# Projections of an attention layer in three float32r passes of split operands instead of a seven-product block scheme

## Chip, cores and metric

The kernel runs on one core of one Trainium2 chip. The metric is the device time of one execution in microseconds, the median of three runs.

## The reference

Two residual layers with layer norms work on `x` of shape 64 x 256 x 512 in float32. The first is a graph layer, the second an eight-head attention with a mask from the same adjacency matrix:

```python
mi = jnp.einsum('bkd,od->bko', x, Wi);  mj = jnp.einsum('bkd,od->bko', x, Wj)
out = deg[None, :, None] * (mi + b) + jnp.einsum('ij,bjo->bio', a, mj)
h = _layernorm(x + out)
...
q, k, v = (split_heads(h @ W.T + b) for W, b in ((Wq, bq), (Wk, bk), (Wv, bv)))
scores = jnp.where(mask, -jnp.inf, jnp.einsum('bhqd,bhkd->bhqk', q, k) * scale)
out = jnp.einsum('bhqk,bhkd->bhqd', jax.nn.softmax(scores, axis=-1), v)
y = _layernorm(h + merge_heads(out) @ Wo.T + bo)
```

The four projections (q, k, v, and o, the output projection) are the part that is changed. Each is a product of 256 x 512 rows per batch with a 512 x 512 matrix.

## The kernel before

The batches are worked on in 32 pairs (`NB = 2`, `NG = 32`). The outer loop is `for g in range(NG - 1)`. One turn holds, in the order in which PE gets it: the attention of pair `g` (scores, exponentials, values, sums `den`) in four steps of two head pairs, with the graph layer of pair `g + 1` (`layer0`) put in between; then the handover; then o of pair `g` and q, k and v of pair `g + 1`, and the first two scores of that pair. The last pair's o is done at the end of the kernel in plain float32 matmuls.

In a projection the two batches of a pair are the two row blocks of one 2 x 2 block matrix, and the weight matrix is another. `pair_steps` does the product of the two in seven block products (Winograd's form of Strassen's scheme) instead of eight; `left_steps` makes the four sums `S1` to `S4` of the left side, `make_factors` the four differences `T1` to `T4` of the weights, once, and stores them in device memory. Each block product is four float32 matmuls of 256 columns, named `st` after their bank in the profile. Each needs one weight block `factor`, 256 KB, which is loaded anew for every pair: 28 loads for a pair. The loads are issued on SP's queue (L442, `bring`) as slots of a ring of nine come free; the order is the list `queue`.

On its way from the graph layer to the projections `h` has to be turned, so that its features lie along the partitions. For the first pair that is done on PE (`h_transpose`). For all others `send_h` writes each row tile to device memory (`h_cols`, L603), reads the whole batch back in another layout (`hB`, L607), and `turn_h` turns it on DVE with a stream transpose of 128 x 1024 (L485).

The handover of a turn starts with the last `values`. `divide_two` copies the unnormalised output from PSUM on ACT, sums the exponentials on PE (`den`), takes the reciprocal on DVE (L886, `rden`), spreads it over the partitions by eight small DMAs on SP (L894, `spread`), and `multiply` on POOL (L848) multiplies. In the same stretch the second batch of the next pair gets the last part of its graph layer: `neighbours` (the matmuls `pa`, whose operands `graph`, `hi` and `lo` are float32r), `take` (L579, add and statistics on DVE, `rstd` on POOL), `give` (L467, normalisation on ACT) and `send_h`. For one batch `take(1)`, `take(0)`, `give(1)`, `give(0)` stand for its two row tiles. `take(1)` of the second batch starts with `add_scaled` (L521).

The order of instructions on an engine is the program's where the code says `in_order`; a scheduler orders the others. [...]

Of the kernel before, what the change touches and what calls it, by code (L numbers as in the profile page):

```python
# [16 lines left out]
P = 128  # L17
# [207 lines left out]
def unshifted_path(ctx, tc, flag, x, adj, wiT, wjT, b0, wqT, bq, wkT, bk, wvT, bv, woT, bo, out):  # L225
# [27 lines left out]
    AHEAD = 8  # L253
# [6 lines left out]
    p4 = ctx.enter_context(tc.tile_pool(name="p4", bufs=4))  # L260
    p6 = ctx.enter_context(tc.tile_pool(name="p6", bufs=6))
    stream = ctx.enter_context(tc.tile_pool(name="stream", bufs=AHEAD + 1))
# [40 lines left out]
    b_bc = p4.tile([P, D], F32, tag="u", name="b_bc")  # L303
# [20 lines left out]
    xT, xS, hT, hS, qT, kT, vv, aoT, oS = ({} for _ in range(9))  # L324


    ident = const.tile([P, P], F32, name="ident")
# [15 lines left out]
    aT = p3.tile([P, NT, N], F32, tag="pk", name="aT")  # L343
    deg = small.tile([P, NT], F32, tag="deg", name="deg")
# [16 lines left out]
    def check_graph():  # L361


        exact = p1.tile([P, NT, N], F32, tag="oS", name="exact")
        in_order(nc.vector.tensor_tensor(exact, aT, graph.bitcast(F32), ALU.not_equal))
        in_order(nc.vector.tensor_reduce(inexact, exact.rearrange("p t n -> p (t n)"), AX.X, ALU.max))
        in_order(nc.vector.tensor_scalar(maskT, aT, 0.0, MASK, ALU.is_equal, ALU.mult))
# [9 lines left out]
    def load_bias(b, name):  # L377
        t = const.tile([P, NC], F32, tag=name, name=name)
        nc.sync.dma_start(out=t, in_=b)
        d = const.tile([P, 2], F32, tag=name + "d", name=name + "d")  # L380
        return t, d

    bq_sb, bqd = load_bias(bq, "bq")
    bk_sb, bkd = load_bias(bk, "bk")

    def bias_steps():
        for t, d in ((bq_sb, bqd), (bk_sb, bkd)):
            in_order(nc.vector.tensor_sub(d, t[:, 2:4], t[:, 0:2]))

    bv_t = small.tile([P, NC], F32, tag="bvt", name="bv_t")  # L390
# [5 lines left out]
    def blocks_of(w):  # L396
        return (w.rearrange("(h c p) (j o) -> p h c j o", h=2, p=P, j=2) if w is woT else
                w.rearrange("(p h c) (j o) -> p h c j o", h=2, p=P, j=2))

    sources = {}  # L400
    for name, w in (("wq", wqT), ("wk", wkT), ("wv", wvT), ("wo", woT)):
        src = blocks_of(w)
        sources[name] = {B11: src[:, 0, :, 0], B21: src[:, 1, :, 0], B22: src[:, 1, :, 1]}


    def load_raw(w, tag):
        raw = p1.tile([P, 2, 2, 2, H], F32, tag=tag, name="raw")
        nc.sync.dma_start(out=raw.rearrange("p h c j o -> p (h c) (j o)"),
                          in_=w.rearrange("(c p) o -> p c o" if w is woT else "(p c) o -> p c o", p=P))
        return raw  # L410

    def make_factors(w, name, raw):
        kept = dram.tile([4, P, 2, H], F32, tag=name, name=name)
        t1, t2, t3, t4 = (p4.tile([P, 2, H], F32, tag="u", name="t") for _ in range(4))
        b11, b12, b21, b22 = (raw[:, h, :, j, :] for h in range(2) for j in range(2))
        for n, (t, p, m) in enumerate(((t1, b12, b11), (t2, b22, t1), (t3, b22, b12), (t4, b21, t2))):
            in_order(nc.vector.tensor_sub(t, p, m))
            nc.sync.dma_start(out=kept[n], in_=t)
        sources[name].update({T1: kept[0], T2: kept[1], T3: kept[2], T4: kept[3]})

    spread = p3.tile([P, NC, P], F32, tag="pk", name="spread")
# [3 lines left out]

    def fold_value_bias(raw):

        pb = score_bank("pb")
        for c in range(NC):
            h, kc = divmod(c, 2)  # L430
            matmul(pb, spread[:, c], raw[:, h, kc].rearrange("p j o -> p (j o)"),
                   start=(c == 0), stop=(c == NC - 1))
        nc.vector.tensor_add(bo_bc, pb, bo_bc)
# [4 lines left out]
    def bring():  # L438
        if queue:
            name, n = queue.pop(0)  # L440
            f = stream.tile([P, 2, H], F32, tag="factor", name="factor")
            nc.sync.dma_start(out=f, in_=sources[name][n])  # L442
            coming.append(f)

    def next_factor():
        f = coming.pop(0)
        bring()
        return f


    def norm_stats(t, order=anywhere):
# [3 lines left out]
        nc.vector.bn_aggr(mv, st)  # L455
        ve = small.tile([P, 1], F32, tag="ve", name="ve")
        nc.vector.tensor_scalar(ve, mv[:, 1:2], EPS, None, ALU.add)
# [3 lines left out]
        nc.gpsimd.tensor_tensor(rstd, ve, mhalf, ALU.pow)  # L461
# [40 lines left out]
    def l0_steps(b, late=False):  # L502
# [21 lines left out]
        def split(t):  # L524
            nc.scalar.copy(k["hi"][:, t, :], k["mj"][:, t, :])
            nc.gpsimd.tensor_tensor(k["lo"][:, t, :], k["mj"][:, t, :], k["hi"][:, t, :].bitcast(F32),
                                    ALU.subtract)
# [13 lines left out]
        def step4():  # L541
            product("y", xS[b]["S2"], T2, True)
            nc.vector.tensor_add(keeper("u2"), banks["y"], k["u1"])

        def step5():
            product("z", xS[b]["S1"], T1, True)
            k["mj"] = p1.tile([P, NT, D], F32, tag="mj", name="mj")
            nc.vector.tensor_copy(k["mj"][:, 1, :], banks["z"])

        def step6():  # L550
            product("y", xS[b]["S3"], T3, False)
            nc.vector.tensor_add(keeper("u3"), banks["y"], k["u1"])
            nc.gpsimd.tensor_tensor(k["mj"][:, 1, :], k["mj"][:, 1, :], k["u3"], ALU.add)
# [34 lines left out]

    def new_h(g):
        hT[g] = p1.tile([P, NC, NB * N], F32, tag="hT", name="hT")  # L590
        hS[g] = pair_blocks(hT[g], "hS")

    def sum_h(g):
        for step in left_steps(hS[g], in_order):
            step()
# [3 lines left out]
    def send_h(b, t):  # L599
        i = b % NB  # L600
        if t == 1:
            h_cols[b] = dram.tile([D // P, N, P], F32, tag=f"h{i}", name="h_cols")
        nc.sync.dma_start(out=h_cols[b][:, t * P:(t + 1) * P, :].rearrange("q p n -> p q n"),  # L603
                          in_=xh[b][:, t, :].rearrange("p (q n) -> p q n", n=P))
        if t == 0:
            hB[b] = p1.tile([P, N // R, P], F32, tag="hB", name="hB")
            nc.sync.dma_start(out=hB[b].rearrange("p a n -> p (a n)"),  # L607
                              in_=h_cols[b].rearrange("q (r a) n -> (q r) (a n)", r=R))

    def turn_h(b):  # L610
        g, i = divmod(b, NB)
        if i == 0:
            new_h(g)
        transposed(hT[g][:, :, i * N:(i + 1) * N], hB.pop(b))
        if i == NB - 1:
            sum_h(g)

    def h_transpose(b, t, borrow=False):
# [4 lines left out]
        pt = (score_banks("pt_h")[:, 0, :] if borrow else bank("pt_h")).rearrange("p (c n) -> p c n", c=NC)  # L623
        for c in range(NC):
            transpose(pt[:, c, :], xh[b][:, t, :].rearrange("p (n c) -> p c n", c=NC)[:, c, :], ident)
        nc.scalar.copy(hT[g][:, :, i * N + t * P:i * N + (t + 1) * P], pt)  # L626
        if t == 0 and i == NB - 1:
            sum_h(g)
# [6 lines left out]
    def pair_blocks(m, tag):  # L635

        s = p1.tile([P, 4, 2, N], F32, tag=tag, name=tag)
        return left_blocks(m[:, 0:2, 0:N], m[:, 2:4, 0:N], m[:, 0:2, N:2 * N], m[:, 2:4, N:2 * N], s)

    def block_product(bank, left, right, flip, first):  # L640


        for m in range(2):
            ms = slice(m * P, (m + 1) * P)
            for kc in range(2):
                lhsT, rhs = (right[:, kc, ms], left[:, kc, :]) if flip else (left[:, kc, ms], right[:, kc, :])
# [471 lines left out]
```

## Time and profile before

| | |
|---|---|
| median of 3 runs | 3070.91 us (3069.15 to 3071.65) |
| profiled execution | 3068.79 us |
| its span | 3066.9 us |
| PE, matmuls | 3036.6 us, 99% |
| DVE | 2178.3 us, 71% |
| POOL | 1519.5 us, 50% |
| ACT | 974.1 us, 32% |
| DMA moved | 447.54 MB, 146 GB/s on average |
| granted TensorE clock | 0.999 |

"Busy" is the union of an engine's instructions. Since matmuls overlap in the array, the mean duration of one is longer than its share of PE's time; what a matmul costs is read from start to start. A duration is in us unless marked ns. The column after the second bar of a group is the time for which the engine stood idle just before these instructions, and who released it. A DMA's time runs from its issue to its landing; DMA issues are listed under the queue of the engine that issues them (SPq for SP).

### The profile page before, as it was taken

The numbers are of one execution on the slowest core, as the hardware profiler recorded it, in microseconds if no ns is written. First come the engines' busy times: TensorE is split into PE (matmuls) and PEld (weight loads), VectorE is DVE, ScalarE is ACT, GpSimd is POOL, SyncE is SP. The second block draws the span as 40 slices with busy tenths as digits, with TensorE's granted clock in tenths as the row PEclk, the third lists the DMA queues.
The fourth block names the chain that finished last, engine by engine and source line by source line (L and its number), as shares of the span: only waits on it lengthen the run. The fifth ranks groups of instructions, "written<-read, shape, count | busy, mean of one in ns | idle before, by whom it ended". The sixth has DMA issues, their size and how long they took to land. (4 is left out here: it accounts for less than half of the span.)

```text
span 3066.9 us, 46810 instructions
## 1 busy us (share of the span) xinstructions
PE 3036.6 (99%) x16646; PEld 2124.6 (69%) x16646; DVE 2178.3 (71%) x3298; ACT 974.1 (32%) x1861; POOL 1519.5 (50%) x1255
## 2 busy tenths in 40 slices
PE   7999999999999999999999999999999999999998
PEld 4667766677766777666776667776677766677665
DVE  6776677766777667777677777677766777767775
ACT  2323333323333333332233332333333333323332
POOL 2544545544545445464454554454544546445453
PEclk9999999999999999999999999999999999999999
DMA  7455544455444555345553445544455444555333
GB/s 255 123 151 159 169 121 136 132 161 166 144 125 127 159 170 155 116 133 154 161 168 119 126 145 160 167 134 134 127 158 170 151 121 128 159 161 166 120 111 96
DMA packets 410411, 447.54 MB, mean 146 GB/s; under 512 B 40896, under 2 KB 300224, under 8 KB 409792
## 3 DMA queue, kind: packets, MB, share of 16 engines
q1 hardware_dynamic: 410176, 444.50, 48.8%
q8 instruction: 136, 2.23, 0.3%
q14 instruction: 99, 0.81, 0.1%
HBM read 340.79 MB, written 70.25 MB: 134 GB/s over the span
## 5 line engine op out<-in xcount | busy, mean ns | idle before, releaser
L461 POOL TENSOR_TENSOR rstd<-ve,mhalf 128x1 f32<-128x1 f32 x256 | 140.5, 552 | 707.3 <-DVE below L459 707.3
L816 POOL TENSOR_TENSOR pk<-pe 128x512 f32<-128x512 f32 x256 | 323.1, 1278 | 322.2 <-ACT pe L813 322.2
L290 PE MATMUL po<-w,xS 128*128 128x512 f32 x1024 | 462.2, 599 | 0.7 <-DVE xS L478 0.7
L290 PE MATMUL st<-hS,factor 128*128 128x256 f32 x2048 | 453.2, 379 | 1.5 <-DVE u L689 1.2
L290 PEld LDWEIGHTS st<-hS,factor 128*128 128x128 f32 x2048 | 388.4, 190 | 56.3 <-DVE xh L744 1.7
L813 ACT ACTIVATE pe<-pe 128x1024 f32<-128x1024 f32 x256 | 270.8, 1058 | 364.4 <-DVE pe L809 364.4
L290 PE MATMUL po<-w,xT 128*128 128x512 f32 x768 | 352.1, 601 | 14.8 <-DVE xS L477 9.3
L290 PE MATMUL st<-hT,factor 128*128 128x256 f32 x1536 | 352.5, 379 | 0.7 <-ACT hT L626 0.7
L290 PEld LDWEIGHTS po<-w,xS 128*128 128x128 f32 x1024 | 189.6, 190 | 235.6 <-issue 206.3
L809 DVE TENSOR_TENSOR pe<-ps,maskT 128x1024 f32<-128x1024 f32 x256 | 298.0, 1195 | 35.4 <-PE ps L290 35.4
L290 PEld LDWEIGHTS st<-hT,factor 128*128 128x128 f32 x1536 | 291.9, 190 | 41.8 <-ACT hT L626 0.9
L886 DVE RECIPROCAL rden<-den 128x256 f32<-128x256 f32 x127 | 222.5, 1752 | 76.6 <-PE den L290 73.6
L290 PEld LDWEIGHTS po<-w,xT 128*128 128x128 f32 x768 | 144.2, 191 | 181.9 <-issue 162.8
L887 POOL TENSOR_TENSOR rtot<-rtot,rden 128x256 f32<-128x256 f32 x127 | 106.8, 841 | 320.1 <-DVE rden L886 320.1
L290 PE MATMUL ps<-qT,kT 64*128 64x256 f32 x2048 | 265.0, 393 | 0.0
L290 PE MATMUL pav<-pe,v_sb 128*32 128x256 f32 x4096 | 248.4, 382 | 1.9 <-ACT pe L813 1.9
L290 PEld LDWEIGHTS ps<-qT,kT 64*128 64x128 f32 x2048 | 184.5, 186 | 78.1 <-issue 38.6
L744 DVE TENSOR_TENSOR xh<-st,xh 128x512 f32<-128x512 f32 x186 | 144.5, 777 | 132.2 <-PE st L290 132.2
L290 PE MATMUL st<-factor,hS 128*128 128x256 f32 x1024 | 234.8, 382 | 0.0
L290 PEld LDWEIGHTS pav<-pe,v_sb 128*32 128x32 f32 x4096 | 119.8, 110 | 164.3 <-issue 95.4
L290 PE MATMUL st<-factor,oS 128*128 128x256 f32 x992 | 224.2, 379 | 0.0
L290 PEld LDWEIGHTS st<-factor,hS 128*128 128x128 f32 x1024 | 192.1, 190 | 35.2 <-issue 10.6
(115 smaller groups left out, 4648.2 us busy)
## 6 DMA issues: line engine op xcount, KB each, us to landing
xB<-in_x_dram SPq DMA_DIRECT2D x256, 128.0 KB, 3.9
xh<-in_x_dram SPq DMA_DIRECT2D x64, 512.0 KB, 4.2
factor<-wq SPq DMA_DIRECT2D x128, 256.0 KB, 4.2
factor<-wk SPq DMA_DIRECT2D x128, 256.0 KB, 2.8
factor<-wv SPq DMA_DIRECT2D x128, 256.0 KB, 2.6
spread<-rden SPq DMA_DIRECT2D x1016, 32.0 KB, 1.9
factor<-wo SPq DMA_DIRECT2D x124, 256.0 KB, 3.2
h_cols<-xh SPq DMA_DIRECT2D x124, 256.0 KB, 3.0
```

The lines of the kernel that those rows point to most:

```text
L290: in_order(nc.tensor.matmul(*args, **kw))
L461: nc.gpsimd.tensor_tensor(rstd, ve, mhalf, ALU.pow)
L744: nc.vector.tensor_add(dst, src, dst)
L809: nc.vector.tensor_add(pe.rearrange("p j t q -> p j (t q)"), ps.rearrange("p j t q -> p j (t q)"), maskT.rearrange("p t q -> p (t q)").uns ...
L813: in_order(nc.scalar.activation(flat, flat, AF.Exp, scale=QSCALE, accum_out=etot[:, NB * g + i, pr:pr + 1]))
L816: nc.gpsimd.tensor_tensor(pk, pe[:, :, 0, :], pe[:, :, 1, :], ALU.add)
L886: nc.vector.reciprocal(rden, den)
L887: nc.gpsimd.tensor_tensor(rtot, rtot, rden, ALU.add)
```

## The change

The seven-product scheme is taken out of all four projections. Each float32 operand is instead split into a head of 12 bits and the rest, and the product is put together from three matmuls of float32r operands. With the head of the left side written A, the rest a, and the head of the weights B, the rest b, a Karatsuba scheme takes three products (head, difference, lifted rest) in place of four. `X` gathers the products of the heads and of the rests, `Y` that of the differences, in two PSUM banks; the result is `X * UP + Y`.

```diff
+    UP, DOWN, LIFT = 1 + 2.0 ** -12, 1 - 2.0 ** -13, 2.0 ** 12
-    AHEAD = 8
+    RING = 5
-    stream = ctx.enter_context(tc.tile_pool(name="stream", bufs=AHEAD + 1))
+    stream = ctx.enter_context(tc.tile_pool(name="stream", bufs=RING))
...
+    def make(f, name, j):
+        head, lift, diff = (f[:, i, :].rearrange("p (c o) -> p c o", c=NC) for i in range(3))
+        low = p3.tile([P, NC, P], F32, tag="lu", name="low")
+        for cs, raw in pieces(name, j):
+            in_order(nc.scalar.activation(head[:, cs], raw, AF.Identity, scale=DOWN))
+            in_order(nc.vector.tensor_sub(low[:, cs], raw, head[:, cs].bitcast(F32)))
+            in_order(nc.scalar.activation(lift[:, cs], low[:, cs], AF.Identity, scale=LIFT))
+        in_order(nc.vector.scalar_tensor_tensor(diff, low, LIFT, head.bitcast(F32), ALU.mult, ALU.subtract))
+        nc.sync.dma_start(out=kept[name][j], in_=f.bitcast(F32))
...
+    def split_head(parts, src):
+        in_order(nc.scalar.activation(parts[0], src, AF.Identity, scale=DOWN))
+    def split_diff(parts, src):
+        in_order(nc.vector.scalar_tensor_tensor(parts[2], parts[0].bitcast(F32), UP, src, ALU.mult, ALU.subtract))
+    def split_low(parts, src, engine):
+        in_order(engine.tensor_tensor(parts[1], src, parts[0].bitcast(F32), ALU.subtract))
...
+    def rows_of_product(banks, parts, t, f, c):
+        X, Y = banks
+        head, low, diff = (d[:, c, t * P:(t + 1) * P] for d in parts)
+        first, end = c == 0, c == NC - 1
+        matmul(X, head, f[:, 0, :], start=first, stop=False, skip_group_check=True)
+        matmul(Y, diff, f[:, 2, :], start=first, stop=end, skip_group_check=True)
+        matmul(X, low, f[:, 1, :], start=False, stop=end, skip_group_check=True)
...
+            dst = store[g][:, m, :]
+            in_order(nc.scalar.activation(dst, X, AF.Identity, bias=bias[:, m:m + 1], scale=UP))
+            in_order(nc.vector.tensor_add(dst, Y, dst))
```

A weight factor is now 128 x 3 x 512, 768 KB, and a projection has four of them, 16 for a pair. They are made on the device in the first pair's pass (`make`) and stored; from then on they are loaded for every pair. The order of the loads is o's four, v's four, then q's and k's in turn; the ring has five slots. o's row tiles of the first batch use all four o factors without giving them back; o's last step (`two`, both row tiles of the second batch) gives one back after each chunk, and each time the next load of the list is issued. v's steps use all four v factors, the last one gives them back. Each q or k step uses one.

```diff
+        def two():
+            banks = [pair(kinds[NT + t]) for t in range(NT)]
+            for c in range(NC):
+                for t in range(NT):
+                    rows_of_product(banks[t], parts, NT + t, coming[0], c)
+                coming.pop(0)
+                bring()
+            for t in range(NT):
+                between[t]()
+                add(1, t, banks[t])
```

`h` is turned and split by row tiles: `hB` is read in two DMAs of 256 KB, and `turn_h` turns 128 x 512 at a time. In SP's order of the changed program the stretch reads: four spreads, `h_cols` twice, the first `hB`, a v factor, the second `hB`, two v factors, then the q and k factors. Half of the last eight spreads of a turn are issued by ACT.

The order in the handover is written out anew, with more of it `in_order`:

```diff
+        values(g, w)
+        values(g, w + 1)
+        low, = three(("v",))
+        aoP[g] = head, low, diff
+        split_low(*ao_parts(g, 0, every), nc.gpsimd)
+        multiply()
+        rden = divide_two(g, w + 1)
+        second_h = turn_h(b1, 0)
+        split_head(*first_h)
+        split_head(*ao_parts(g, 1, upper))
+        split_head(*second_h)
+        run([neighbours, take1])
+        split_diff(*ao_parts(g, 1, upper))
+        split_low(*ao_parts(g, 1, upper), nc.gpsimd)
+        run([give1, send1])
+        multiply()
+        split_head(*ao_parts(g, 1, lower))
+        run([take0, give0, send0])
+        split_diff(*first_h)
+        split_diff(*ao_parts(g, 1, lower))
+        split_low(*ao_parts(g, 1, lower), nc.gpsimd)
...
+        o[0]()
+        split_diff(*second_h)
+        split_low(*second_h, nc.gpsimd)
+        run([*o[1:], v[0], v[1], v[3], v[2], end[0], q[0], end[1], k[0], end[2], q[1], end[3], k[1], end[4]])
```

In the graph layer's `l0_steps` one copy out of PSUM of the second batch goes from DVE to ACT, and one subtraction of `split` from POOL to DVE. The last pair's attention and its o are as before.

## The prediction

> **What bounds the kernel now.** I read the engine shares and queue totals of the page first, then the waits of PE, the groups kept apart by shape, and the timeline of PE and of SP across one handover from a batch pair's attention to the next pair's projections.
>
> ```profile
> PE 3036.6 (99%) x16646; PEld 2124.6 (69%) x16646; DVE 2178.3 (71%) x3298; ACT 974.1 (32%) x1861; POOL 1519.5 (50%) x1255
> ...
> q1 hardware_dynamic: 410176, 444.50, 48.8%
> ```
>
> PE is the only full engine. The list of who PE waited for confirms that this is work and not stall: nothing but single waits, all of them in the first 100 us.
>
> ```profile
> PE po L290 <- DVE xS L477: 9.3, 1, 9.3
> PE po L290 <- DVE xT L485: 2.8, 1, 2.8
> ...
> PE st L290 <- DVE u L689: 1.2, 1, 1.2
> ```
>
> So PE time saved is kernel time saved, as long as PE goes on never waiting. Next, what a matmul costs. Busy time overlaps, so I read start to start in PE's timeline:
>
> ```profile
> 326.87 0.62 PE L290 MATMUL den<-pk,ones 128*32 128x256 f32 x8
> 327.41 1.99 PE L290 MATMUL st<-factor,aoT 128*128 128x256 f32 x8
> 329.05 0.58 PE L290 MATMUL pa<-hi,graph 128*128 128x512 f32 x1
> 329.48 0.39 PE L290 MATMUL pa<-lo,graph 128*128 128x512 f32 x1
> ...
> 330.88 0.40 PE L290 MATMUL pa<-lo,graph 128*128 128x512 f32 x1
> ...
> 334.56 5.34 PE L290 MATMUL st<-hT,factor 128*128 128x256 f32 x24
> 339.74 1.89 PE L290 MATMUL st<-factor,aoT 128*128 128x256 f32 x8
> ```
>
> A float32 matmul leaves two records (1024 of `po<-w,xS` for 512 in the program). Twenty-four `st` records take 339.74 - 334.56 = 5.18 us, 0.216 us each. The `pa` matmuls have float32r operands: one record each, (330.88 - 329.48)/6 = 0.234 us for 512 columns. In float32, two records of 512 columns take about 0.90 us.
>
> SP's timeline after the same handover shows the second resource that matters:
>
> ```profile
> 329.88 4.94 SPq L894 DMA_DIRECT2D spread<-rden  x8
> ...
> 336.44 0.38 SPq L603 DMA_DIRECT2D h_cols<-xh  x1
> ...
> 338.64 0.44 SPq L603 DMA_DIRECT2D h_cols<-xh  x1
> 339.94 0.33 SPq L442 DMA_DIRECT2D factor<-wq  x1
> 342.86 0.33 SPq L607 DMA_DIRECT2D hB<-h_cols  x1
> 343.29 0.86 SPq L442 DMA_DIRECT2D factor<-wq  x2
> ```
>
> SP stands at the `hB` read until the `h_cols` write has landed, and the factor loads stand behind it (339.94 to 343.29). Today that is free: the ring brings eight factors ahead, 1.73 us of PE work each.
>
> **What the Trainium skill says.** "FP8 and Floating Point Precision", TensorE Precision Notes, has four passes for true FP32 and a reduced form truncated to FP22; the trace agrees in ratio (0.90 to 0.234). "DMA: Bandwidth & Descriptors", Anatomy of one DMA, says that DMA engines do not wait on semaphores and that the issuing sequencer waits before dispatch; the SP rows above are that wait. Its Specifications give a fabric ceiling of 435 GB/s; the window 17 to 30 us, with the engines nearly always busy, moves about 410.
>
> **The change, part by part.**
>
> *Matmuls.* Removed: 7112 `st` records (the six `st` groups) x 0.216 = 1536 us. Added: per pair 192 float32r matmuls of 512 columns (48 for each of q, k, v, o; 31 pairs have o, 32 the others), 6096 x 0.234 = 1426 us. Net -109 us; per pair with o, 224 x 0.216 - 192 x 0.234 = 3.4. Each has its own weight load, as in `pa`, so I use that pitch. The ends are 0.225 (half of a float32 record of 512 columns, if a record is two passes), which gives 55 us more, and 0.252, where the whole gain is gone.
>
> *Vector work.* DVE loses the Winograd combinations (about 19 us a pair by their rows) and gains 12 evictions of 0.69, 4 of 1.43 and the splits (about 24): 68 to 72 us of a 95 us pair. ACT goes from 30 to some 37, POOL from 47 to about 46. By share none becomes the bound; their order in the handover matters below.
>
> *Factor loads.* 880 loads of 256 KB become 492 of 768 KB: 231 to 387 MB. The ring holds five. When o starts it holds four `wo` and the first `wv`; loads `wv` 1 to 3 wait for the slots that o's last step frees, one per 1.4 us, and v's first step wants them 0.7 us apart right after it.
>
> *The handover,* time 0 being when PE goes from `den` to `pa` (327.41 above is the same point). PE: `pa` to 1.9, o row tiles to 4.7 and 7.5, o's last step to 13.1, the first v step to 15.9 if nothing is late. The vector chain: reciprocal 0.5 to 2.3 (1.77), half a transpose to 3.4 (half of 2.15), `add_scaled` to 4.4 (0.95), then the first `take`, whose variance is ready at 6.1 (add 0.69, statistics 0.69, three short ones); the new `split_diff` stands between the takes (0.95), so the second variance comes at 8.9. POOL: low of the first batch 0 to 2.6, multiply to 3.9, rstd 6.1 to 6.7, low to 8.0, multiply to 9.3, rstd to 9.9. ACT: four spread DMAs, then heads; apply to 7.9, head 10.0, apply 11.1. In SP's order, which I read in the changed program: four spreads; `h_cols` at 8.0 and 11.2; `hB` at 11.6; `wv` 1 at 12.0; the second `hB`, which waits for the second `h_cols` (3.0 median): 14.2; behind it `wv` 2 at 14.7 and `wv` 3 at 15.1. The second `h_cols` went out at 338.64 - 327.41 = 11.2 before, too, so the chain is no longer than now; what is new is that PE wants `wv` 3 at 15.2.
>
> No 768 KB load exists yet. Its neighbours:
>
> ```profile
> hB<-h_cols SPq DMA_DIRECT2D x62, 512.0 KB, 3.5
> ...
> wo_sb<-in_woT_dram SPq DMA_DIRECT2D x1, 1024.0 KB, 5.4
> ```
>
> That is 4.45 by interpolation, 3.7 from the fastest `hB` (3.1) plus 256 KB at 410 GB/s; I take 4.1. Then `wv` 1 lands at 16.1, `wv` 2 at 19.3 (its `hB` goes ahead of it), `wv` 3 one transfer later (768 KB / 410 GB/s = 1.9) at 21.2. PE ends the first v step at 21.9 instead of 15.9: **6.0 us lost per pair**, in 31 pairs 186 us. Smaller lateness before (low of o's last chunk 0.4, low of h 0.5) is inside this, since the landing times do not depend on it. The ends are 4.5 (fast landing, apply 1 us earlier) and 7.5 (4.45 and `h_cols` at 4.2, as at 342.86).
>
> *ACT issues half of the last spreads.* An ACT issue has no row; SP's has 0.59 median. Two queues give 2.4 us instead of 4.9; both ends (0.3, 1.2 each) leave `multiply` behind POOL's own low. Hidden, 0.
>
> *Prologue.* 16 factors are made before the first scores, each DVE 0.69 + 0.95 with two ACT passes; the first v step needs four while PE has only the last layer-0 product: about 7 us idle against the waits of 1 to 2 us now. I take +6, range 0 to 15. The weight factor loads in q and k (one per 2.8 us, 280 GB/s, five ahead) are hidden; pinned order and attention stage: no new operand on PE's path, 0, ends -0.3 and +0.5 a pair.
>
> Sum: the profiled execution's 3068.8 - 109 + 186 + 6 = 3152; the median of the runs is 2 above it: **3155**.
>
> **Rivals.** (1) *Bandwidth only, faster.* If `h` is stored earlier than I chain it, only the ring's size counts: `wv` 1 leaves at 9.2, when o's last step has used its first chunk; a fixed part near 2 (4.1 less 1.9 of transfer), the `hB` reads ahead of it (1.0) and three transfers of 1.9 end at 17.9: 2.7 lost a pair, 3052. Below 3.3 lost a pair the change gains; that is `wv` 3 landing before 18.5. For it: DMA runs at 410 in bursts. Against: the two `hB` reads are ahead in SP's order, and 11.2 is measured. (2) *Everything hidden, faster:* 2968, if the loads land as fast as they are wanted; against it are 2.4 MB in 6 us. (3) *Slower still.* PE idles some 5 us in 7; the skill's "TensorE: Matmul & The Clock Gate", Part 1, has the clock halved after an idle window of about 3.4 us. No such idle lies in this trace (granted clock 0.999). Half a window of work lost, 1.7 us a pair, gives 3207; a DVE queue that runs late costs the same sort of sum. (4) *The pitch is not 0.234:* at 0.252 nothing is saved, 3263; `pa` speaks against it.
>
> **Numbers.** The stall as worked out 0.62 (3107 to 3200), rival 1 0.15, rival 2 0.06, rivals 3 and 4 0.13, a balance of both 0.04. Range 3035 to 3215 leaves out rival 2 and part of 3 and 4. 0.2% is about 6 us, roughly what runs of this kernel can tell: faster 0.21, same 0.04, slower 0.75.
>
> **What would show it.** Right: PE's waits list `factor` loads of `wv` with some 90 waits and 100 to 190 us; SP's timeline has the `wv` loads right after the second `hB`; 12 projection matmuls take 2.8 us; the PE share falls to about 93%. Wrong: no DMA among PE's waits, or a `wv` load issued before 12 us, or a pitch away from 0.234.

## The result, and the profile after

The changed kernel takes **3240.45 us** (median of 4 runs, 3237.68 to 3243.24) against 3070.03 for the kernel before on the same chip: a ratio of **1.0555** (95% interval 1.0537 to 1.0573), so it is slower. The forecast was 3155 with a range of 3035 to 3215: the side and the mechanism were right, but the loss is twice the one forecast (170 us by the medians, 174.6 by the spans of the two profiled executions, against 84) and the time is outside the range.

The page of the changed kernel, at the places shown before:

```profile
PE 3042.7 (94%) x15630; PEld 1948.8 (60%) x15630; DVE 2375.3 (73%) x3411; ACT 1162.4 (36%) x2022; POOL 1542.8 (48%) x1221
...
q1 hardware_dynamic: 307376, 602.68, 53.4%
...
factor<-wv SPq DMA_DIRECT2D x124, 768.0 KB, 6.3
...
h_cols<-xh SPq DMA_DIRECT2D x124, 256.0 KB, 2.4
hB<-h_cols SPq DMA_DIRECT2D x124, 256.0 KB, 2.9
```

PE is no longer full: 94% of a longer span. Its busy time has not fallen, although 1016 records are gone. Most of both comes from one place. The list of what PE waited for (us in total, times, the longest) now has a DMA at its head, where before it held 2.7 us in all after the first 100 us:

```profile
PE pxy L290 <- DMA factor<-wv: 99.2, 93, 2.7
PE px L290 <- POOL v L604: 29.2, 62, 0.6
PE pxy L290 <- POOL hL L604: 19.1, 31, 0.7
PE pxy L290 <- POOL v L604: 11.8, 31, 0.4
```

Ninety-three waits are three for each of 31 turns. PE's timeline shows the three in one turn; T = 0 of this turn, the start of `pa`, is at 356.61. Columns: start, duration, operation, and in brackets the idle time before it with what ended it.

```profile
371.94 0.39 PE L290 MATMUL pxy<-factor,hA 128*128 128x512 f32 x1
372.17 0.39 PE L290 MATMUL pxy<-factor,hD 128*128 128x512 f32 x1
373.17 0.50 PE L290 MATMUL pxy<-factor,hL 128*128 128x512 f32 x1 [0.61 <-POOL hL L604]
...
375.43 0.80 PE L290 MATMUL pxy<-factor,hA 128*128 128x512 f32 x1 [1.76 <-DMA factor<-wv]
376.02 0.63 PE L290 MATMUL pxy<-factor,hD 128*128 128x512 f32 x1
376.45 0.63 PE L290 MATMUL pxy<-factor,hL 128*128 128x512 f32 x1
377.96 0.80 PE L290 MATMUL pxy<-factor,hA 128*128 128x512 f32 x1 [0.88 <-DMA factor<-wv]
379.84 0.79 PE L290 MATMUL pxy<-factor,hA 128*128 128x512 f32 x1 [0.23 <-DMA factor<-wv]
...
381.29 0.63 PE L290 MATMUL px<-factor,hA 128*128 128x512 f32 x1
```

The first v step starts at T+15.3 and ends at T+24.7; twelve matmuls at the steady pitch need 2.7 us. Only 2.9 us of that step are shown as load waits, and 0.6 as a wait for `hL`. Most of the rest is hidden in the durations: from 375.4 on, matmuls start 0.43 us apart instead of 0.23, and the first one after a wait 0.59. The windows of the same turn say why. Columns: stretch, its length, busy time and count of PE, weight loads, DVE, ACT and POOL, granted TensorE clock, DMA share, GB/s.

```profile
core 0: us, PE busy (x) PEld busy (x) DVE busy (x) ACT busy (x) POOL busy (x), PEclk, DMA share, GB/s
356.60:371.90 15.30, 14.01 (x60) 10.30 (x57) 14.77 (x22) 4.83 (x9) 12.74 (x11) 1.00 0.25 66
371.90:375.40 3.50, 1.16 (x4) 0.38 (x3) 2.18 (x4) 0.63 (x1) 1.21 (x1) 1.00 1.03 377
375.40:382.30 6.90, 5.76 (x12) 3.64 (x13) 5.39 (x9) 1.23 (x2) 0.00 (x0) 0.51 0.75 309
382.30:400.00 17.70, 17.70 (x80) 14.61 (x79) 8.64 (x23) 6.84 (x13) 2.43 (x5) 1.00 0.63 246
```

After 3.5 us in which PE was busy a third of the time, the granted clock is 0.51 for 7 us. This stretch of lower clock comes in all 31 turns, 218 us of it in total. So a PE that reads 5.76 us busy of 6.90 is doing less than half of that work. The DMA columns of the second and third rows are the transfers that it waits for. SP's timeline has their issue:

```profile
365.64 3.84 SPq L621 DMA_DIRECT2D h_cols<-xh  x2
369.58 0.45 SPq L625 DMA_DIRECT2D hB<-h_cols  x1
370.12 0.40 SPq L428 DMA_DIRECT2D factor<-wv  x1
371.77 0.32 SPq L625 DMA_DIRECT2D hB<-h_cols  x1
372.18 0.86 SPq L428 DMA_DIRECT2D factor<-wv  x2
```

The order is the one that was forecast: store, store, read, load, read, load, load.

**Where the 174.6 us are.** I cut the span at each handover's `den` on PE. Up to the first one: 138.1 us before, 156.0 after (+18). Thirty turns: 94.43 us each before, 99.52 after, 30 x 5.09 = +153. After the last: +4. Within a turn the three attention stages are the same to 0.05 us (11.29, 10.1 and 11.29); the whole difference lies between the handover's `den` and the next turn's first `den`.

### The profile page after: what moved, and what is told of

Its sections match the earlier page's. It is cut to its first block, busy times and chain, and to the rows that moved or that the text cites. A ratio compares the mean times of both kernels' runs of the same rounds, so it can differ in the third digit from the quotient of the medians.

```text
span 3241.5 us, 43618 instructions
## 1 busy us (share of the span) xinstructions
PE 3042.7 (94%) x15630; PEld 1948.8 (60%) x15630; DVE 2375.3 (73%) x3411; ACT 1162.4 (36%) x2022; POOL 1542.8 (48%) x1221
## 5 line engine op out<-in xcount | busy, mean ns | idle before, releaser
L459 POOL TENSOR_TENSOR rstd<-ve,mhalf 128x1 f32<-128x1 f32 x256 | 167.9, 656 | 874.6 <-DVE below L457 855.5
L689 DVE TENSOR_TENSOR kT<-py,kT 128x512 f32<-128x512 f32 x128 | 88.1, 689 | 193.4 <-ACT kT L688 193.4
L290 PE MATMUL pxy<-factor,hA 128*128 128x512 f32 x256 | 133.2, 520 | 103.1 <-DMA factor<-wv 99.2
L598 ACT ACTIVATE hA<-hF 128x512 fp32r<-128x512 f32 x124 | 77.7, 627 | 413.4 <-DVE hF L483 266.6
L865 POOL TENSOR_TENSOR rtot<-rtot,rden 128x256 f32<-128x256 f32 x96 | 70.2, 731 | 322.1 <-DVE rden L853 322.1
L465 ACT ACTIVATE xh<-xh,shift,rstd 128x512 f32<-128x512 f32 x256 | 208.7, 815 | 8.6
L451 DVE BATCH_NORM_STATS2 st<-xh 128x6 f32<-128x512 f32 x256 | 176.2, 688 | 3.4
L604 POOL TENSOR_TENSOR v<-aoT,qT 128x512 fp32r<-128x512 f32 (+1 forms) x93 | 178.3, 1917 | 0.1
L290 PE MATMUL px<-hA,factor 128*128 128x512 f32 x640 | 176.4, 397 | 1.6 <-DMA factor<-wk 0.8
L290 PE MATMUL py<-hD,factor 128*128 128x512 f32 x640 | 172.1, 391 | 1.6 <-ACT kT L688 1.5
```

What stands on the lines that cost most here:

```text
L290: in_order(nc.tensor.matmul(*args, **kw))
L451: order(nc.vector.bn_stats(st, t))
L459: order(nc.gpsimd.tensor_tensor(rstd, ve, mhalf, ALU.pow))
L465: order(nc.scalar.activation(t, t, AF.Identity, bias=shift, scale=rstd))
L598: in_order(nc.scalar.activation(parts[0], src, AF.Identity, scale=DOWN))
L604: in_order(engine.tensor_tensor(parts[1], src, parts[0].bitcast(F32), ALU.subtract))
```

## The experiments

Times and ratios are against the kernel before on the same chip. "Period" is the mean of 30 turns, from handover to handover, in the one execution of a run that was profiled; the times are medians of several executions. T is the start of `pa`.

| run | us | ratio (95%) | period |
|---|---|---|---|
| before | 3070.03 | 1 | 94.43 |
| after | 3240.45 | 1.0555 (1.0537 to 1.0573) | 99.52 |
| e1_fill | 3241.77 | 1.0562 (1.0544 to 1.0579) | 99.16 |
| e2_order | 3243.05 | 1.0566 (1.0548 to 1.0584) | 99.53 |
| e3_order_low | 3233.41 | 1.0529 (1.0512 to 1.0547) | 99.20 |
| e4_inter | 3137.21 | 1.0223 (1.0206 to 1.0240) | 96.05 |
| e5_order_swap | 3155.17 | 1.0282 (1.0265 to 1.0299) | 96.49 |
| e6_seq | 3099.13 | 1.0092 (1.0075 to 1.0108) | 94.93 |
| e7_seq_low | 3083.41 | 1.0043 (1.0026 to 1.0060) | 94.53 |
| e8_seq_early | 3101.22 | 1.0101 (1.0084 to 1.0118) | 94.87 |
| e9_one_factor | 3068.73 | 0.9999 (0.9991 to 1.0008) | 93.94 |
| e10_ring6 | 3242.26 | 1.0560 (1.0543 to 1.0576) | 99.51 |
| e11_ring6_all | 3130.69 | 1.0199 (1.0185 to 1.0213) | 95.71 |
| e12_ring6_room | 3237.50 | 1.0540 (1.0525 to 1.0555) | 99.01 |

### Is the halved clock the cost? (e1_fill)

PE gets matmuls to do while it would stand idle: the first chunk of v's first step is repeated three times, and two more fillers go into the next step's banks.

```diff
+            if (i, t) == (0, 0) and g:
+                early[g] = pair("M")
+                for _ in range(3):
+                    rows_of_product(banks, hP[g], 0, coming[0], 0)
...
+                if (i, t, c) == (0, 0, 2) and g:
+                    for _ in range(2):
+                        rows_of_product(early[g], hP[g], 1, coming[0], 0)
```

> Added work, nothing moved: in each of 31 turns v's first chunk is multiplied three more times while PE would stand waiting for the second v factor (9 matmuls), and twice more into the next step's banks ahead of the third chunk (6 matmuls), 15 x 0.23 = 3.4 us of extra PE work a turn. The results are overwritten by the real products. Theory (the idle of some 4 us around the v factor loads halves the granted clock, which costs some 13 matmuls 0.2 us each): the loads land when they landed, T+18.7, T+21.4 and T+23.2 from the start of pa, the clock stays at 1.00 and v's chunks go at 0.228 instead of 0.43, so v's first step ends 0.4 to 1 us earlier and the following matmuls are at full clock at once: 1 to 2.5 us a turn less, 3165 to 3210 against 3240. Rival (the clock is lowered by something else, power or the float32r stream itself): the 0.43 pitch stays after the fillers and the time goes up by up to 3.4 us a turn, 3240 to 3350.

The clock came back, and the time did not. The same stretch of the span (1.2 us earlier against this run's T), and the head of PE's waits:

```profile
375.40:382.30 6.90, 4.85 (x22) 3.68 (x21) 5.85 (x9) 0.88 (x2) 0.00 (x0) 1.00 0.91 373
```
```profile
PE pxy L290 <- DMA factor<-wv: 60.3, 39, 2.4
```

The granted clock is 1.00 here and the mean of the run 0.993 (0.962 after; 5 of the 31 turns still have a short stretch at half clock), yet the period fell by 0.36 us only, and the time is the same. Even the 0.36 is not clear of the spread: the profiled execution is the fastest of this run's four, that of the changed kernel the slowest of its four. Fifteen extra matmuls, 3.4 us a turn, cost nothing, since PE would have waited for the third load anyway: the first v step still ends at about T+24.7. That the idle PE causes the low clock is shown: with more of the same matmuls the clock stays up, so neither power nor the float32r stream lowers it. The 1 to 2.5 us a turn that I had given for it did not come. One thing limits what this says of the price: in e1 the third load lands later than in the changed kernel, at T+23.9 on average against T+23.2, which takes up the 0.8 us that its last three matmuls gain. With the landing held still the low clock would be worth some 1.1 us a turn (an estimate: 0.36 and the 0.7 of the later landing), out of 5.1. Why the load lands later is open.

### Can the loads go ahead of `h`'s reads? (e2_order, e3_order_low, e5_order_swap)

e2 pins SP's order: all three v loads before the second `h_cols` store and the two `hB` reads.

```diff
-        run([take0, give0, send0])
+        run([take0, give0])
...
-    def o_steps(g, kinds, between):
+    def o_steps(g, kinds, between, after_loads):
...
+                if c == 2:
+                    after_loads()
```

> SP's order alone is changed: the three v factor loads go ahead of the second h_cols store and of both hB reads. Theory (a v load is late because it stands behind hB reads that wait for h_cols to land): the loads are issued at about T+9.7, 11 and 12.5, land by T+14.5, 16 and 17.5, the first v step ends at about T+18.5 instead of T+24.7 and the clock stays high: 6 to 7 us a turn less, 3020 to 3060. Rival (bandwidth and the small ring: the loads can't land in time anyway, and the hB reads are late in their place): PE waits for hD or hL of the second batch in the third v step instead, and less than 3 us a turn is won, 3150 to 3240.

No gain: another wait took the place of the one removed. PE's waits, then SP's and DVE's timelines:

```profile
PE pxy L290 <- DMA factor<-wv: 50.4, 43, 2.7
PE px L290 <- DVE xh L713: 44.6, 27, 3.1
...
PE pxy L290 <- DVE xh L714: 28.6, 19, 1.7
```
```profile
365.83 4.10 SPq L428 DMA_DIRECT2D factor<-wv  x3
370.02 0.39 SPq L621 DMA_DIRECT2D h_cols<-xh  x1
370.51 5.94 SPq L625 DMA_DIRECT2D hB<-h_cols  x2
```
```profile
376.84 1.13 DVE L483 STREAM_TRANSPOSE hF<-hB 128x512 f32<-128x512 f32 x1 [5.94 <-DMA hB<-h_cols]
...
379.88 0.68 DVE L713 SCALAR_TENSOR_TENSOR xh<-px,xh 128x512 f32<-128x512 f32 x1
380.60 0.69 DVE L714 TENSOR_TENSOR xh<-py,xh 128x512 f32<-128x512 f32 x1
```

DVE stands 5.94 us at the transpose of the late `hB`. Behind it, in its own order, stand o's evictions (L713 and L714), and PE waits for the banks that they would empty.

e3 adds to e2 that the low parts of o's second batch are made on DVE instead of POOL:

```diff
-        split_low(*ao_parts(g, 1, upper), nc.gpsimd)
+        split_low(*ao_parts(g, 1, upper), nc.vector)
...
-        split_low(*ao_parts(g, 1, lower), nc.gpsimd)
+        split_low(*ao_parts(g, 1, lower), nc.vector)
```

> e2 with the two subtractions split_low of the second batch of o on DVE instead of POOL. Theory (the waits of PE for POOL's low in o, 0.4 + 0.3 + 0.6 as idle and some 1.9 us in start to start, sit on the path once the v loads do not end last): 0.5 to 1.5 us a turn less than e2, that is 15 to 45 us. Rival (DVE is then late with its evictions and diffs, each low costing it 0.7 to 1.4 us): no difference to e2 or up to 30 us more.

It is 0.33 us a turn: POOL's lateness is not what decides, as long as DVE and the loads are later.

e5 adds to e2 that o's evictions stand ahead of the transposes:

```diff
+            for t in range(NT):
+                add(1, t, banks[t])
             for t in range(NT):
                 between[t]()
-                add(1, t, banks[t])
```

> e2 with one change in DVE's order: the two evictions of o's last step stand ahead of the turning and splitting of h of the second batch, not behind. Theory (in e2 the reads of h came late in the place of the v loads, and DVE stood before a late hF with o's evictions queued behind it, so PE waited for o's PSUM banks): the waits of PE for L713 and L714 (2.5 us a turn in e2) go; PE waits for the splits of h instead where it needs them, 1.5 to 3 us later, so 0 to 2 us a turn are won: 3180 to 3243. Rival (the banks were a symptom, h itself ends last): PE's wait moves whole to the splits, no gain within 10 us of e2's 3243.

The L713 and L714 waits are gone from PE's list, and the period falls by 3.0 us against e2. At the head of the list now stand 52.8 us in 39 waits for v factors. So the reading of e2 holds: SP's order alone gained nothing, SP's order with the evictions moved gains 3.0 us. The evictions moved alone were not run.

### Can PE use each factor twice as it lands? (e4_inter)

The first two v steps are done together, chunk by chunk, in two pairs of banks:

```diff
+            for c in range(NC):
+                for t in range(NT):
+                    rows_of_product(banks[t], hP[g], t, coming[c], c)
```

> The changed kernel with the first two v steps (row tiles 0 and 1 of the first batch) interleaved by chunk, so that each v factor is used for six matmuls instead of three before the next is wanted; loads and their order stay. Theory (PE waits for the landing times): the last v factor lands at T+23.2 as before, but by then half of the second step is done as well: 3 x 0.68 = 2 us a turn less, plus the share of the half clock: 3140 to 3190. Rival (the second step's banks or evictions hold it up): no gain, 3230 to 3250.

3.5 us a turn, 103 us by the medians, without a DMA moved. Work that doesn't need the next factor was put between the landings.

### What do the landings cost, by themselves? (e9_one_factor)

```diff
-                rows_of_product(banks, hP[g], NT * i + t, coming[0 if last else c], c)
+                rows_of_product(banks, hP[g], NT * i + t, coming[0], c)
```

> Only the address of an operand changes: in v's first three row tiles every chunk uses the factor of chunk 0, which was loaded in the turn before, so no v step that comes first waits for a load (what is left out: those three row tiles of v are multiplied by one quarter of the weights four times; all loads, all instructions and their order stay). Theory (the landings of the second to fourth v factors set when the first v step ends, T+24.68 where 12 matmuls of 0.2275 after its start at T+15.33 would end at T+18.1): the load waits of 3.2 us a turn and the half clock go together, the step ends at about T+18.5, the period goes from 99.52 to about 93.4, and the time to 3241 - 31 x 6.1 = 3052, with some 10 us more off the prologue, where v no longer waits for the later factors: 3040 to 3055. Rival (the next batch element's h is late next: its hB read lands about T+16.5 and its split on DVE stands behind o's evictions): the third v step waits for DVE instead and the period falls only to 95 to 97, 3110 to 3165.

This is the experiment that settles the cause: every instruction and every transfer stays, and only the wait for the three later factors goes. The three loads land at T+18.3, 21.1 and 23.0 on average, as in the changed kernel (18.6, 21.3 and 23.2). The list of PE's waits has no v load in it, and the step runs at the full pitch (T is 621.67 in a turn of this run):

```profile
PE px L290 <- POOL v L604: 29.1, 61, 0.7
PE pxy L290 <- POOL hL L604: 19.1, 31, 0.6
PE pxy L290 <- DVE xh L714: 14.1, 30, 1.7
```
```profile
636.96 0.39 PE L290 MATMUL pxy<-factor,hA 128*128 128x512 f32 x1
...
638.20 0.50 PE L290 MATMUL pxy<-factor,hL 128*128 128x512 f32 x1 [0.62 <-POOL hL L604]
638.54 0.40 PE L290 MATMUL pxy<-factor,hA 128*128 128x512 f32 x1
...
640.63 0.39 PE L290 MATMUL px<-factor,hA 128*128 128x512 f32 x1
```

The first v step ends at T+18.96 on average instead of T+24.66, 5.70 us earlier, and the period is 93.94 instead of 99.52, 5.58 less. The half clock does not appear in any turn. The whole slowdown against the kernel before is gone: the ratio is 0.9999. The rival, that the other batch's `h` would be late next, is refuted as to its size: the third v step does not wait for `h`, and the period lies below the 95 to 97 that the rival gave. I had expected some 16 us less: 0.5 us a turn goes to a new wait of v's banks for o's eviction (the third row), and the prologue gave 4 us rather than 10.

### All of it in a sequence (e6_seq, e7_seq_low, e8_seq_early)

e6 is e4 and o's evictions first, and SP's order is the store and two loads, one read, the other store, the third load, the other read:

```diff
+                if c == 1:
+                    read_h(NB * (g + 1) + 1, 1)
+                    store_h(NB * (g + 1) + 1, 0)
+                if c == 2:
+                    read_h(NB * (g + 1) + 1, 0)
...
+            for t in range(NT):
+                add(1, t, banks[t])
             for t in range(NT):
                 between[t]()
-                add(1, t, banks[t])
```

> e4 (two v steps interleaved by chunk), with o's evictions ahead of h's splits as in e5, and SP's order written so that no load stands behind a wait that is longer than its own: first h_cols store, v factors 1 and 2, first hB read, second h_cols store, v factor 3, second hB read, q factor. Theory (the two late chains, v factors and h, fit side by side if each transfer leaves when its own input is there): the last v factor lands near T+19 instead of T+23, the two v steps end near T+21 to T+22, h is split by then: 2 to 3 us a turn less than e4, 3040 to 3080. Rival (410 GB/s carry 3.1 MB of v factors and h no sooner; what one gains the other loses): 3120 to 3150 as e4.

e7 is e6 with e3's edit:

> e6 with POOL's two split_low of o's second batch on DVE, as in e3. Theory (POOL's lateness ahead of v now adds to the turn, since the v loads no longer cover it): 0.5 to 1.3 us a turn less than e6, 15 to 40 us. Rival (the v loads still end last, or DVE is late): within 10 us of e6.

e6 has a period of 94.93 and e7 of 94.53, against 94.43 before: in the turns, nearly the whole loss is recovered with the loads still waited for. Here e3's edit is worth 0.40 us a turn. Left over in e7, 1.4 us a turn for the loads:

```profile
PE pxy L290 <- DMA factor<-wv: 42.1, 32, 2.7
PE px L290 <- DVE v L604: 19.8, 31, 0.7
```

What keeps e7 above before is mainly the 18 us in front of the first handover. e8 is e6 with the first factors made before the first `h_transpose`:

```diff
+    for _ in range(RING):
+        bring()
     h_transpose(0, 1)
...
-    for _ in range(RING):
-        bring()
```

> e6 with the first five weight factors made before the first h is turned instead of after it (prologue only). Theory (the prologue is 18 us longer than before because PE waits for the makes on ACT and DVE, and idles into the half clock): 4 to 10 us less than e6, all of it before the first handover. Rival (the makes only move ahead of h's own split on the same engines): within 3 us.

The first handover comes at 158.7 us, in e6 at 157.0. No gain: PE then stands 10.7 us once at an `h_transpose` for DVE, instead of at v for the factors. The work of making them lies on DVE and ACT either way. A part of the 18 us can be read from the clock. From 40 to 62 us of the span, where the changed kernel makes its first factors and PE waits for them, the first row is the changed kernel, the second the kernel before:

```profile
40.00:62.00 22.00, 15.82 (x40) 9.14 (x40) 14.50 (x25) 9.57 (x17) 4.39 (x4) 0.69 0.51 202
40.00:62.00 22.00, 19.69 (x75) 13.30 (x74) 16.30 (x35) 10.56 (x21) 7.80 (x7) 1.00 0.67 221
```

Up to the first handover the changed kernel has 20.5 us at half clock, the kernel before 3.4. That can account for 8 to 9 of the 18 us at most (an estimate: half of the difference); in e9 it is 6.8 us, and there the first handover comes 4 us earlier. How the rest divides is open.

### A sixth buffer (e10_ring6, e11_ring6_all, e12_ring6_room)

```diff
-    RING = 5
+    RING = 6
...
-    p6 = ctx.enter_context(tc.tile_pool(name="p6", bufs=6))
+    p6 = ctx.enter_context(tc.tile_pool(name="p6", bufs=5))
...
-        rden = p2.tile([P, N], F32, tag="rden", name="rden")
+        rden = p1.tile([P, N], F32, tag="rden", name="rden")
```

> One more factor buffer (six for five), so that one v factor more is already there when o begins to give buffers back, and the three late loads become two. The room comes from one x buffer less (a turn's second x load moves behind the out stores), a single-buffered rden, and sums of the exponentials kept for one batch element only (what is left out: the overflow check looks at the last element's sums alone). Theory (landings decide, about 2 us apart): the last landing comes one load earlier, the first v step ends at about T+22.5 rather than T+24.7, and the period falls by 2 to 3 us to 96.5 to 97.5, 3150 to 3180. Rival A (the landings are late because of the queue in SP and the traffic of hB, not because of their number): the two loads still land at T+19 and T+21.5 but the last is now the second; the same number, so told apart only by the landing times. Rival B (the single-buffered rden and the later x load cost as much as the buffer brings): period 99 or more, with waits on rden or on x new in the lists.

PE's timeline, where T is 651.19, has one landing less in the step:

```profile
669.80 0.50 PE L290 MATMUL pxy<-factor,hA 128*128 128x512 f32 x1 [0.99 <-DMA factor<-wv]
...
672.44 0.61 PE L290 MATMUL pxy<-factor,hA 128*128 128x512 f32 x1 [1.67 <-DMA factor<-wv]
```

The step ends at T+22.54 on average, 2.1 us earlier, as the theory had it, and the stretch behind the handover is 1.76 us shorter. But the third attention stage is 1.74 us longer (13.03 for 11.29), and the period stays. Rival B had named this sort of cost. DVE's waits and its timeline in that stage, which starts with `den` at 439.36:

```profile
DVE rden L853 <- DMA spread<-rden: 49.8, 25, 3.4
```
```profile
441.85 1.76 DVE L853 RECIPROCAL rden<-den 128x256 f32<-128x256 f32 x1 [1.64 <-DMA spread<-rden]
443.52 2.29 DVE L771 TENSOR_TENSOR pe<-ps,maskT 128x1024 f32<-128x1024 f32 x2
445.73 0.68 DVE L542 TENSOR_TENSOR u<-po,u 128x512 f32<-128x512 f32 x1
```

The reciprocal can't write `rden` until the spread DMAs of the division before have read it. The row is not in the list after, where `rden` has two buffers: there the reciprocal starts 0.7 us after `den`, here 2.5. Layer 0's sum (L542), which PE waits for, comes 6.4 us after `den` instead of 4.6.

> The sixth factor buffer together with the four edits of the earlier run (first two v steps interleaved by chunk, SP's sequence of h stores, v loads and hB reads, o's evictions ahead of h's splits on DVE, the low parts of o on DVE), which gave a period of 94.53 with 1.4 us a turn still waiting for v factors. What is left out is the same as for the sixth buffer alone. Theory: these waits go and the period falls by 1 to 2 us to 92.5 to 93.5, so the time to 3025 to 3055, below the kernel before (3070), with the prologue still 18 us longer. Rival: with the loads gone from the end of the handover, h's splits on DVE and the v low on POOL end last; the period stays at 94 to 94.6 and the time at 3070 to 3085, no gain over before.

Both expectations missed. The load waits are gone from PE's list, but against e7 the stretch behind the handover is only 0.71 us shorter, while the third stage is 1.88 longer (13.17), and what follows the thirty turns takes 7.6 us more.

e12 finds the room elsewhere, to test my reading at that time, that the later x load was to blame:

```diff
-    p3 = ctx.enter_context(tc.tile_pool(name="p3", bufs=3))
+    p3 = ctx.enter_context(tc.tile_pool(name="p3", bufs=2))
...
-        spread = p2.tile([P, 2, N], F32, tag="spread", name="spread")
+        spread = p1.tile([P, 2, N], F32, tag="spread", name="spread")
...
-            order(nc.vector.tensor_add(keeper("u3"), banks["y"], k["u1"]))
+            k["u3"] = k["u1"]
+            order(nc.vector.tensor_add(k["u3"], banks["y"], k["u1"]))
```

> The version with all edits and six factor buffers once more, with the room found elsewhere, so that the second x load of a turn stays where it was: single buffers for rden and spread, two in place of three for layer 0's kept products (u3 is written over u1), and the sums of the exponentials added up turn by turn on POOL (one small instruction a turn; the overflow check is complete). Theory (the late x load alone cost the 1.95 us a turn that the second attention stage grew by with six buffers; the handover stage keeps its gain of 0.64 over the run with five): attention stages back to 11.29, 10.09 and 11.29, period 94.53 - 0.64 = 93.9, and the time 3083 - 31 x 0.64 = 3063, from 3055 to 3070: 0.995 to 1.000 of before. Rival (the single buffers or the two kept products hold back layer 0 or the division): an attention stage stays above 11.5, the period is 94.5 or more, and the time 3080 to 3130.

That theory fell. With the x load back in its place the third stage is 13.40, and DVE waits 65.1 us in 30 waits for the spreads. All three six-buffer runs have the single `rden`, and all three have that wait, of 2.0 to 2.2 us; that it is the cause is read from the traces, since no run has six buffers and two `rden`. In e12 the stretch behind the handover is 3 us longer than in e11 as well; which of its smaller pools does that was not separated. No run here beats the kernel before; e7 comes nearest of those that compute all of it.

## Why the prediction was right, and where it was wrong

The step that failed is the price of the handover: 6.0 us lost a pair were forecast, 9.8 were measured. The path was right (PE waits for v's second to fourth factor, which are issued behind the reads of `h`), but the loads were issued later, landed more slowly, and left PE at half clock, which the forecast had priced only in a rival. Against the forecast's terms, the sum of what was measured is:

| term | forecast, us | measured, us |
|---|---|---|
| matmuls | -109 | -149 |
| lost in the handover, 31 turns | +186 (6.0 each) | +304 (9.8 each) |
| prologue | +6 | +21 |
| sum | +83 | +176 |

The measured handover is the period's 5.09 and the 4.7 that 192 matmuls at the measured pitch save against 224 records of 0.216. The prologue is its 18 us and the 3.5 that its own matmuls save, which stand in the first row. The spans differ by 174.6: the last turn lost 4 us rather than 5.

**Matmuls: right in kind, 40 us too dear.** The float32r matmul with its own weight load has a pitch of 0.227 to 0.228 (four in 0.907 us in the q steps), not the 0.234 read from `pa`. The lower end that I had named, 0.225, was the better guess, though its working was not right: read from start to start, two float32 records of 512 columns take 0.86 us in the kernel before (four `po` records from 19.75 to 21.47), not 0.90, which is busy time, and half of one is 0.215. Rival 4 is refuted.

**The order in SP and the timetable: right, each step late.** The first v load was forecast for T+12.0 and went out at 13.5; the other two 14.7 and 15.1, measured 15.6 and 16.0. Two durations in the chain to the stores were taken too short: `add_scaled` takes 1.53 us rather than 0.95, and `rstd` on POOL, taken as 0.55, takes 1.0 in this stretch, twice (its median over the kernel is 0.55). POOL's first low part takes 2.85 rather than 2.6 too, but it is not in that chain: POOL stands idle for 2.56 us ahead of the first `rstd`.

**The landing: the term that was mis-sized.** I had the factors at T+16.1, 19.3 and 21.2. In the turn above they can be used at 18.8, 21.35 and 23.2: 5.3, 5.75 and 7.2 us after their issue instead of 4.1, 4.6 and 6.1. The 4.1 was interpolated from an `hB` read and one load at the end of the kernel before, neither of which had such company: here two `hB` reads and a q factor share the queues at 377 GB/s. In e2, where the v loads go out ahead of the reads, the first takes 4.5 us to land and the third 6.05 (means of 31 turns), against 5.0 and 7.2 in the changed kernel, which speaks for the company as a part of it; it was not tested by itself. The 1.9 us for one more transfer held (21.3 to 23.2). So the first v step ends at 24.7 rather than 21.9. Of these 2.8 us, 0.9 are later issue, 1.1 slower landing, and 0.8 the last three matmuls at half clock. 2.8 x 31 = 86 us; another 1.0 a turn (31 us) lies outside this: 0.4 in the tail of the low clock behind that step, and 0.4 because the 15.9 was worked out with the longer pitch. With the matmuls' 40 taken off and the prologue's 15 added that is 92 us, the difference between the two sums.

**"Smaller lateness before is inside this": right for the sum, but it is three times as large.** The forecast had 0.9 us of it. Without load waits the step ends at 18.96 (e9), not at my 15.9, since POOL's low parts and `hL` make PE wait 1.9 us a turn by the list (60 us in 31 turns), 2.7 in the turn above read from start to start. All of it is covered while the last landing is later. It is what is late next once the loads are early, and it is most of why e9 is level with before and not 2968: of the 9.8 us lost in the handover e9 gets back 5.6, and 4.2 stay.

**Rival 3: its event came, its price did not.** The Trainium skill's "TensorE: Matmul & The Clock Gate", Part 1, has the clock halved after an idle window of about 3.4 us; the trace shows the halved clock in all 31 turns (0.51 in the one above), but without a fully idle window, and here the measurement decides: in the 3.4 us before the clock fell PE was busy 18 to 55% of the time, and its longest single gap was 2.7 us. The forecast's "no such idle lies in this trace" was a misreading as well: in the kernel before the window 21 to 30 us has a clock of 0.81, around a wait of PE of 2.76 us. Most of the low clock lies under the waits for loads: e1 gained 0.36 us a turn, and the price is some 1.1 by the estimate above, not 1.7. **Rivals 1 and 2** needed a landing before 18.5 or no wait at all; e9 shows the second with the waits removed, and it gives 3069, not 2968, mostly for the reason above. With 4.2 us a pair still lost in e9, rival 1's 2.7 could not have come from earlier landings alone.

**Costed at nothing, and rightly as far as the traces show:** ACT's four spread issues (one row of 2.44 us, as worked out; `multiply` starts when POOL's own low part ends), the weight loads of q and k (under 1 us of waits for `wk`, none for `wq` of note), the attention stages (the same to 0.05 us). **Prologue:** +21, more than three times my value and above its range's end. Four of it go where v doesn't wait for the later factors (e9); the half clock, which was not in the term, is at most 8 to 9 of it.

**Readings that were off without moving the sum.** It is the stretch 21 to 30 us of the kernel before that moves 418 GB/s; 17 to 30 us as a whole moves 335. The sum for DVE comes to 73 us a pair by its own parts, not 68 to 72, and 74 were measured.

The signs named beforehand came as told: 93 waits and 99 us for `wv`, three loads around the second `hB`, twelve matmuls in 2.7 us, PE at 94%. They tell the mechanism, not the size: the list of waits holds 99 us (3.2 a turn) of the 173 (5.6 a turn) that e9 gets back, because the half clock and the slow starts after a wait count as busy time; the other 131 of the 304 stay in e9.

## What to carry to other kernels

When a cheaper product needs more bytes, don't set traffic against the mean bandwidth: look for the one place in a turn where the new bytes can't be asked for early, and price it as issue time plus landing under the load of that very window. A wait list understates such a stall where the engine's clock drops. Work that can go on with what has landed (two row tiles per factor) repairs more (3.5 us a turn) than a new order of issue alone (nothing), and an in-order queue passes lateness on to whatever stands behind it, so moving a load past a read moved the wait into o's evictions.

## What was not expected of the hardware

- The granted TensorE clock fell to 0.51 for 7 us after 3.5 us in which PE was busy a third of the time; over the 31 turns PE had been busy 18 to 55% of the 3.4 us before. With 15 filler matmuls it stayed at 1.00 (in the same stretch) and the time did not change.
- A float32r matmul of 512 columns with a new weight load each time starts every 0.227 to 0.234 us; at the low clock every 0.43.
- The same 768 KB load takes 5.3 to 7.2 us to land beside 256 KB reads, with the queues moving 309 to 377 GB/s.
- The POOL instruction for `rstd`, 128 x 1, takes 0.55 us by the median of the changed kernel's 256, and 1.0 in the handover (0.99 and 1.00 in the turn above); why is open.
